# A scheduled four-direction state-space scan on one core: unread products in TensorE's idle stretches, and a limit on second PE stages in a slot

## The chip, the cores and the metric

The kernel runs on one core of a Trainium2 chip. The metric is the device time of one execution in microseconds (us). The engines are called PE (TensorE, with PEld for its weight loads), DVE (VectorE), ACT (ScalarE), POOL (GpSimd) and SP (which issues DMAs here).

## The reference, cut to what matters

The input is 32 images of 128 channels by 32 x 32 points. Four layers are added to it in turn: a 3 x 3 convolution, a Mamba block over four directions, an attention map with two short Mamba blocks, and a small simulated circuit. Nearly all of the time goes to the second layer. Its core, for each direction of each image, is

```
def step(h, inp):
    dt_t, B_t, C_t, u_t = inp
    dA = jnp.exp(dt_t[..., None] * A)
    h = dA * h + (dt_t * u_t)[..., None] * B_t[:, None, :]
    y = jnp.einsum('bdn,bn->bd', h, C_t)
    return (h, y)
```

It runs over 1024 positions with 256 channels (two halves of 128) and 16 states. In front of it stand a projection, a four-tap causal convolution with silu, a projection to B, C and the rate, and a softplus; behind it a skip term, a silu gate and an output projection.

## The kernel before, in words

**Steps.** One direction of one image is a "way" of 32 steps: two halves by 16 states, each step over a 128 x 1024 tile. 32 images give 128 ways, 4,096 steps; the third layer adds 64. `Steps.run` emits one loop iteration per step i, by hand and in this order: on ACT `decay` of step i+3 (L616, the tile `da`); on PE `spread` of step i+1, which puts the row of B into the PSUM tile `bu`; on DVE `scan` (L660, reads `da` and `bu`, writes `hh`) and then `input` of step i+1 (L652, multiplies `bu` by `du`); the stages that the plan hands out; on ACT `scale` for step i+4 (L645); on POOL `weigh` (L669, multiplies `hh` by the row of C, which SP loads as `cc`); and on PE `add` of step i-2 (L705, sums `hh` into `y` by eight transposes).

Two kinds of steps differ in `spread`. In 11 of 32 (`TURNED`) it is eight transposes of `but`, which ACT has scaled (L630), and DVE has no `input`. In the other 21 it is two bf16 products with a selector (L636), and DVE does `input`. `bu` has two buffers, so the products of step i+1 may begin when the scan of step i-1 is done, and the scan of step i+1 needs them one step later: PE's lead over DVE is at most about one step.

**Stages.** All other work of the second layer and its neighbours is cut into `Stage` objects with costs in us for PE, ACT, POOL and DVE: for the next way the projections (`project`, L263), `small` (L282), `keep`, `turn`, `split`, `unturn`, the rate chain (`rate` L360, `expo`, `rounded`, `log`, `lost`, two `whole`, `weighed`), `turns` (L417); for a finished one `gate` (L464), `finish` (L442) and the way out (L1004); for the next image `layer0` with six `conv` stages of 2.6 us of PE (L952). `Plan.slot(i, steps)` is asked once per step. It sorts the streams of stages by slack, and runs at most one stage of each stream if buffers, gaps and a credit per engine allow. `load_of` gives the step's own costs: PE 1.55 us in a plain step, 2.05 with a turned step following, 1.05 more in two steps of 16.

**Buffers.** PE stages write to the PSUM tag `mm`, which has two buffers. Their reading by ACT (or DVE) is held back by `later` and emitted by `flush`, mostly in the next iteration. `mm()` flushes first when two are outstanding[...].

**Tables.** ACT switches between silu and exp/log with a table load: `silu` marks the table as lost, `exps` (L751) loads it again.

## Time and profile before

| | |
|---|---|
| median of 3 runs | 15195.86 us (15194.75 to 15206.05) |
| profiled execution, own time | 15187.89 us |
| its span | 15185.8 us |
| mean granted PE clock | 0.920 |
| busy: DVE, PE, POOL, ACT | 13587.7, 13220.0, 12554.2, 12296.5 us |
| scans (L660) | 4160, 2279 ns each |
| `input` (L652) | 2752, 1212 ns each |
| ACT table loads, L745 and L751 | 481 each, 1283 ns each |

The profile is of one execution. Each engine's row gives its busy time; "idle before" is the engine's time without work ahead of an instruction, with what ended it. PEclk is the clock that PE was granted, as a share of full speed. The span and the execution's own time differ by 2.1 us, which lies outside the first and last instruction.

### The profile page before, as it was taken

What the parts mean: (1) busy time and instruction counts of PE and PEld (TensorE: products, weight loads), DVE (VectorE), ACT (ScalarE), POOL (GpSimd) and SP (SyncE); (2) the same over time, 40 slices, a digit from 0 to 9 for tenths busy, and PEclk for the clock granted to TensorE, in tenths of its full rate; (3) what the DMA queues carried; (4) which work ended last, traced back from release to release, by engine and by line L of the source; (5) the groups of instructions that cost most, each with busy time, mean ns of one, the idle gap of its engine ahead of it and who ended that gap; (6) DMA issues with size and microseconds to landing.
All of it is one profiled execution on the core that took longest, in us unless ns stands there. A gap on an engine that the chain in (4) does not pass through costs nothing.

```text
span 15185.8 us, 197534 instructions
## 1 busy us (share of the span) xinstructions
PE 13220.0 (87%) x70318; PEld 8502.3 (56%) x70318; DVE 13587.7 (89%) x8999; ACT 12296.5 (81%) x21240; POOL 12554.2 (83%) x6433
## 2 busy tenths in 40 slices
PE   7888888888888888888888888888888888888776
PEld 4555555555555555555555555555555555555431
DVE  5999989999999999999899999999999998999887
ACT  6888888888888888888888888888888888888632
POOL 5888888888888888888888888888888888888730
PEclk8999999999999999999999999999999999999877
DMA  3444444444444444444444444444444444444321
GB/s 108 160 156 155 155 153 154 157 158 156 155 156 154 153 156 158 156 156 155 153 153 156 158 156 156 154 155 154 158 159 156 155 156 154 154 159 157 132 96 57
DMA packets 633029, 2277.42 MB, mean 150 GB/s; under 512 B 76808, under 2 KB 80280, under 8 KB 631912
## 3 DMA queue, kind: packets, MB, share of 16 engines
q1 hardware_dynamic: 625128, 2246.09, 42.9%
q0 software_dynamic: 4608, 16.78, 0.3%
q8 instruction: 554, 9.08, 0.2%
q14 instruction: 435, 3.56, 0.1%
q10 hardware_dynamic: 2304, 1.90, 0.0%
HBM read 2221.24 MB, written 43.25 MB: 149 GB/s over the span
## 4 chain that ended last, share of the span: by engine, by line
PE 30%; DVE 24%; ACT 22%; issue 16%; POOL 6%; DMA 1%; DVEq 0%; POOLq 0%; ACTq 0%; SPq 0%
DVE hh L660 14%; DVE bu L652 8%; PE y L705 7%; ACT da L616 7%; ACT but L645 6%; PE mm L263 6%; POOL hh L669 4%; PE bu L636 3%; PE bu L630 3%; PE mm L282 3%; PE mm L952 2%; ACT L751 2%; ACT L745 2%; PE mm L360 1%; PE y L684 1%
## 5 line engine op out<-in xcount | busy, mean ns | idle before, releaser
L669 POOL TENSOR_TENSOR hh<-hh,cc 128x1024 f32<-128x1024 f32 x4160 | 9771.9, 2366 | 1771.3 <-DVE hh L660 1058.4
L660 DVE TENSOR_TENSOR_SCAN hh<-da,bu 128x1024 f32<-128x1024 f32 x4160 | 9411.1, 2279 | 587.1 <-PE bu L630 199.1
L705 PEld LDWEIGHTS y<-cbig,hh 128*128 128x128 f32 x33280 | 4056.6, 150 | 1797.2 <-issue 1264.0
L705 PE MATMUL y<-cbig,hh 128*128 128x128 f32 x33280 | 4754.6, 290 | 194.5 <-POOL hh L669 193.8
L616 ACT ACTIVATE da<-dt,m_na 128x1024 f32<-128x1024 f32 x4096 | 4606.1, 1144 | 329.4 <-DVE hh L660 322.6
L652 DVE TENSOR_TENSOR bu<-du,bu 128x1024 f32<-128x1024 f32 x2752 | 3334.4, 1212 | 747.3 <-PE bu L636 745.7
L645 ACT ACTIVATE but<-dut,bt 128x128 f32<-128x128 f32 x11264 | 3433.6, 392 | 0.0
L636 PE MATMUL bu<-parts,sel 48*128 48x512 bf16 x5504 | 1762.2, 402 | 604.8 <-DVE hh L660 597.0
L263 PE MATMUL mm<-hpad,m_wc 128*128 128x512 f32 x4096 | 2038.6, 621 | 102.4 <-ACT relu L369 68.4
L630 PE MATMUL bu<-cbig,but 128*128 128x128 f32 x11264 | 1613.7, 291 | 379.4 <-DVE hh L660 315.3
L630 PEld LDWEIGHTS bu<-cbig,but 128*128 128x128 f32 x11264 | 1391.7, 152 | 447.7 <-issue 292.0
L263 PEld LDWEIGHTS mm<-hpad,m_wc 128*128 128x128 f32 x4096 | 704.7, 191 | 899.2 <-issue 747.9
L636 PEld LDWEIGHTS <-sel 48*128 48x128 bf16 x5504 | 322.4, 95 | 1115.7 <-DVE hh L660 647.8
L385 POOL TENSOR_TENSOR w<-w,du 128x1024 f32<-128x1024 f32 x260 | 613.8, 2361 | 29.7 <-ACT w L378 29.7
L282 PE MATMUL mm<-uc,m_xw 128*128 128x512 f32 x1024 | 602.4, 719 | 30.4 <-ACT sz L745 21.9
L745 ACT ACT_TABLE_LOAD x481 | 617.1, 1283 | 8.5
L751 ACT ACT_TABLE_LOAD x481 | 617.1, 1283 | 8.5
L422 ACT COPY dut<-mm 128x512 f32<-128x512 f32 x512 | 294.9, 576 | 405.4 <-PE mm L417 405.1
L684 PEld LDWEIGHTS y<-m_skip,uc 128*128 128x128 f32 x4096 | 552.1, 212 | 125.9 <-issue 76.7
L389 POOL TENSOR_TENSOR dt<-dt,w 128x1024 f32<-128x1024 f32 x260 | 615.1, 2366 | 0.3
L394 POOL TENSOR_TENSOR du<-dt,uc 128x1024 f32<-128x1024 f32 x260 | 614.3, 2363 | 0.3
L389 POOL TENSOR_TENSOR dt<-dt,relu 128x1024 f32<-128x1024 f32 x260 | 613.9, 2361 | 0.0
(227 smaller groups left out, 10502.0 us busy)
## 6 DMA issues: line engine op xcount, KB each, us to landing
cc<-rows SPq DMA_DIRECT2D x4160, 512.0 KB, 3.8
xt<-in_x SPq DMA_DIRECT2D x32, 512.0 KB, 5.9
x<-xt SPq DMA_DIRECT2D x32, 512.0 KB, 3.5
xt<-x SPq DMA_DIRECT2D x32, 512.0 KB, 3.5
out<-xt POOLq DMA_DIRECT2D x32, 512.0 KB, 2.9
rows<-dbl SPq DMA_DIRECT2D x130, 64.0 KB, 4.1
stats<-st SPq DMA_DIRECT2D x32, 36.0 KB, 1.5
means<-stats SPq DMA_DIRECT2D x1, 1152.0 KB, 7.1
```

The costliest lines, as they stand in the source:

```text
L263: nc.tensor.matmul(self.view(ps), m.wc[:, v, j, h * P : (h + 1) * P], self.taps(j, c), start=(j == 0), stop=(j == 3),)
L282: nc.tensor.matmul(ps, m.xw[:, h], self.uc[h][:, cs], start=(h == 0), stop=(h == 1))
L389: nc.gpsimd.tensor_tensor(self.dt[h], self.dt[h], t[name], op)
L616: k.nc.scalar.activation(t, w.dt[h], AF.Exp, scale=w.m.na[:, h, n : n + 1])
L630: k.nc.tensor.matmul(t[:, b * P : (b + 1) * P], but[:, b], k.ident, start=True, stop=True, is_transpose=True,)
L636: k.nc.tensor.matmul(t[:, cs], k.sel[:, n], w.parts[:, cs], start=True, stop=True)
L645: k.nc.scalar.activation(t[:, b], w.dut[h][:, b], AF.Copy, scale=w.bt[:, b, n : n + 1])
L652: k.nc.vector.tensor_tensor(t, w.du[h], t, ALU.mult)
L660: k.nc.vector.tensor_tensor_scan(way(t), way(self.da.pop(i)), way(self.bu.pop(i)), 0.0, ALU.mult, ALU.add)
L669: k.nc.gpsimd.tensor_tensor(t, t, self.cc.pop(i), ALU.mult)
L705: k.nc.tensor.matmul(self.y[g][: w.bl, b], t[:, at], k.ident, start=False, stop=(n == DS - 1 and b == w.per - 1), is_transpose=True,)
L745: self.nc.scalar.activation(*args, AF.Silu, **kw)
```

## The change

Three things are new. `Plan.slot` keeps `busy`, the costs of the step and of the stages handed out in it, and passes over a stage if a PE stage is already in the slot, if the sum for PE would go over 3.6 us, and if its stream has slack over 1.2. It returns PE's and DVE's sums. `Steps.run` keeps `late`, an account of PE's lag: PE's sum less 1.1 times DVE's, never below zero after an iteration. At the end of an iteration, when the account says that PE is ahead by more than 1.2 us, `Kernel.idle` issues products of 48 x 512 bf16 that nothing reads, one for each 0.25 us of the rest, into a buffer of the tag `mm`, unless two users of that tag are outstanding.

```diff
--- before.py
+++ after.py
...
         self.credit = [min(c + self.SLOT - own, self.SLOT) for c, own in zip(self.credit, steps)]
+        busy = list(steps)
...
             stage = s["left"][0]
+            if slack(s) > 1.2 and busy[0] > steps[0] and busy[0] + stage.cost[0] > 3.6:
+                continue
             if i < max(stage.at, s["last"] + stage.gap):
                 continue
...
             self.credit = [c_ - c for c, c_ in zip(stage.cost, self.credit)]
+            busy = [b + c for b, c in zip(busy, stage.cost)]
...
+        return busy[0], busy[3]
...
+        late = 0.0
         for i in range(len(steps) + 2):
...
             if self.has(i):
-                plan.slot(i, self.load_of(i))
+                pe, dve = plan.slot(i, self.load_of(i))
+                late += pe - 1.1 * dve
             self.scale(i + 4)
             self.weigh(i)
             self.add(i - 2)
+            if self.has(i + 2):
+                late += k.idle(-late - 1.2)
+            late = max(late, 0.0)
             self.load(i + 3)
...
+    def idle(self, us):
+        each = 0.25
+        n = int(us / each)
+        if n < 1 or len(self.waiting) + len(self.behind) + self.open + bool(self.single) > 1:
+            return 0.0
+        ps = self.psm.tile([P, 512], F32, tag="mm", name="unread")
+        for _ in range(n):
+            self.nc.tensor.matmul(
+                ps, self.half[: 3 * DS], self.sel[:, :4].rearrange("p n d -> p (n d)"),
+                start=True, stop=True,
+            )
+        return n * each
```

## The prediction

> **What bounds the kernel now.** I read the page's busy shares and clock row first, then who waited for whom, then stretches and the timeline of one image.

> ```profile
> PE 13220.0 (87%) x70318; PEld 8502.3 (56%) x70318; DVE 13587.7 (89%) x8999; ACT 12296.5 (81%) x21240; POOL 12554.2 (83%) x6433
> PEclk8999999999999999999999999999999999999877
> ...
> DVE bu L652 <- PE bu L636: 745.7, 519, 87.2
> DVE hh L660 <- PE bu L630: 199.1, 170, 3.2
> ...
> PE y L705 <- POOL hh L669: 193.8, 181, 3.0
> ```

> DVE paces the loop. By the timeline a plain step lasts 3.54 us and one before a turned step 2.20, with no wait in it; 32 steps (21 and 11) make 98.6 us, an image 394. Scans of the trace are 442 us apart per image, so 48 us of an image are something else: about 21 us of other DVE work and some 27 us in which DVE waits for PE. The two DVE rows say so: less the one wait of 87.2 us, which lies outside the images, they are 857 us, 27 per image. This is the prize, 860 us at most. The tenths of the clock row hide that PE ran at half speed for a part of it: the mean is 0.92.

> The waits come in clusters. Two of them, in one image (times on the left, waits in brackets):

> ```profile
> 2448.94:2457.19 8.25, 4.65 (x25) 2.31 (x24) 8.08 (x8) 7.77 (x15) 7.19 (x4) 0.91 0.54 191
> 2457.19:2469.81 12.62, 12.62 (x55) 8.42 (x56) 9.32 (x8) 4.43 (x11) 12.38 (x8) 0.78 0.29 96
> ...
> 2455.99 1.03 PE L636 MATMUL bu<-parts,sel 48*128 48x512 bf16 x2 [3.08 <-DVE hh L660]
> 2456.95 3.78 PE L282 MATMUL mm<-uc,m_xw 128*128 128x512 f32 x4
> 2460.81 2.98 PE L684 MATMUL y<-m_skip,uc 128*128 128x128 f32 x16
> 2464.36 1.23 DVE L652 TENSOR_TENSOR bu<-du,bu 128x1024 f32<-128x1024 f32 x1 [1.23 <-PE bu L636]
> ...
> 2549.70 0.33 PE L442 MATMUL mm<-cbig,carry 128*128 128x128 f32 x1 [2.28 <-ACT uc L745]
> 2555.54 1.12 PE L360 MATMUL mm<-dbl,m_dw 32*128 32x512 f32 x2 [1.51 <-ACT dut L422]
> 2556.59 0.30 PEld L952 LDWEIGHTS mm<-xpad,w 128*128 128x128 f32 x2 [0.76 <-ACT relu L369]
> 2560.87 1.23 DVE L652 TENSOR_TENSOR bu<-du,bu 128x1024 f32<-128x1024 f32 x1 [5.92 <-PE bu L636]
> ```

> First: in two slots without PE stages (2448.94 to 2457.19) PE is busy 4.65 of 8.25 us; then the clock is down to 0.78, L282 takes 3.78 us (four of them at full speed about 2.0), and DVE waits. Second: a slot got `turn`, `rate` and a `conv` at once. Each in turn waits until ACT has read one of the two `mm` buffers: 2.28 + 1.51 = 3.8 us of PE, and the third one's weight load 0.76 (its product starts right behind the one before). DVE then waits 5.92.

> [...] I cut it into the stretches of 3.41 us in which its clock changes, and took each product's array time from the spacing of its like (0.109 us for 128 f32 columns, 0.216 for 512 bf16). Of 221 stretches at full clock in which the array was filled under 40%, 204 were followed by half clock; from 40 to 50%, 41%; above 80% practically none of 2,152. Back to full it goes only from a well filled stretch: none of 132 under 70%, 81% of 399 above 80%. A plain slot without a stage fills 8 x 0.109 + 2 x 0.216 = 1.30 of 3.54 us, 37%: it is just too empty. [...] of 440 stretches in which other products filled under a tenth, only 22% were followed by half clock. [...]

> **The change, part by part.** The built program shows what the plan does.

> *Unread products.* 2,520 of them, in 799 of 4,160 slots, mostly four at a time. The nearest row is L636, with the same 48 x 512 bf16: spacing 0.216 us at full clock, 0.43 at half. So 2,520 x 0.216 = 544 us more of PE, 17 us per image. Four add 0.86 us: the plain empty slot goes from 37 to 61% filled, out of the zone that surely lowers the clock. They stand at the end of an iteration, behind `add`, ahead of the next `spread`; that one waits for a scan's end anyway (L636 <- DVE was 3.08 us above), and this wait covers them. Without that cover they would cost what they last, up to 0.86 us a slot.

> *The limit of 3.6.* Slots with two or more PE stages fall from 725 to 500, slots with over 3.6 us for PE from 1,137 to 916. PE's work per image is unchanged (374 us of stage costs). As projections also run closer together, ACT's pairs of table loads fall from 481 to 420: 122 x 1.283 = 157 us off ACT, which is not the bound. I count 0 for it, and up to 30 us, because DVE rows that wait for ACT are small (`but` 15.6 us). Nothing is added to SP's or POOL's queues; POOL's rate chain only moves by some slots. `keep`, whose DMA writes the rows that `cc` loads read, moves from slot 7 to 8 or from 5 to 9 of a way and is needed in slot 29.

> *By cluster of an image.* Slots are counted from the image's first step; "before" is DVE's wait for PE, averaged over 30 images; "after" is what PE's sum leaves over DVE's pace less one step of lead, with half a microsecond where a low clock is still possible.

> - 19 to 26: 4.35, 4.35, 3.80, 3.30 in a row, then 4.20, 3.80, 3.30; now 4.35, 4.35, 2.05, 3.30. Before 2.9, after 0.4.
> - 32 to 36: two empty slots, then 4.65 and 5.25 at half clock; now 3.30, 3.30, 4.35, 2.90, 2.05, never empty. Before 2.6, after 0.2.
> - 45: before 1.1; now filled, after 0.4.
> - 52 to 57: before 1.8, after 0.1.
> - 60 to 71, six `conv`: before 10.7, of which about 4 are the buffer waits. Now one `conv` has a slot with at most a `turn`, so these go. But the delayed projections now meet the `conv`: PE's sum is 49.8 us, DVE's pace 37.1 plus 1.5 for two L964; 11.2 less a step's lead of 3.5 leaves 7.7. With something for buffers, after 8.5.
> - 72 to 83: before 5.6. The account still says that PE lags there (by up to 9.6 us in slot 71, although DVE has waited that off), so nothing is filled and the clock may fall. After 4.
> - 91 to 94, 103 to 104, 123 and smaller ones: before 3.3, after 1.1.

> Sum before 28, after 14.7. For new waits that I don't see I take 2.5: 10.8 us less per image, times 31.5 (the first image lacks some) 340 us. From the profiled execution's 15187.9 us that gives 14,848; the median of the runs stands 8 us higher, so 14,855.

> **Rivals.** A change of 0.2%, 30 us, is about what a measurement of this kernel can tell from none.

> *Levelling and clock both work, as above:* 14,680 to 15,000. Chance 0.45.

> *The fillers don't hold the clock:* 61% is in the band (50 to 80%) in which about one stretch in nine still led to half clock, and slots with one filler stay near 43%. Then the limit alone works: of 13.3 us saved about 7 per image without the clusters at 33, 45, 91 and 123: 14,970. Chance 0.16.

> *Waits move instead of going:* PE's work is the same, and the conv cluster grows. If slots 60 to 83 take back 7 to 8 of the other clusters' 9.5 us, 15,100 remains (0.15 for a gain of over 30 us), or nothing (0.07). For it: 49.8 us of PE there against 44.4 before.

> *Slower, by fillers in the way:* the account takes costs at full clock and knows nothing of POOL. `add` waits for POOL (193.8 us in 181 times), the fillers stand behind it, and the next `spread` behind them; at half clock four of them last 1.7 us. It decides from the point where 340 of their 544 us, 63%, are no longer covered. If all are in the way the time is 15,195.9 + 544 - 340 = 15,400; with most of them and a grown conv cluster, 15,300. Against it: they are given only where the slot has over a microsecond to spare, and DVE's scan was what PE waited for in 912 us (L636 597.0, L630 315.3). Chance 0.17.

> **The numbers.** Likeliest 14,855, own range 14,680 to 15,000. The range for 8 in 10 reaches over the second and third cases into no change and the mildest losses: 14,680 to 15,220. Faster 0.45 + 0.16 + 0.15 = 0.76, same 0.07, slower 0.17.

> **What would show it.** Right: L652's wait for L636 falls from 746 to some 450 us and L630's row from 199 to about 100; granted clock 0.95 or more; 420 table loads per line; PE busy higher by about 500 us and DVE's unchanged; the unread products idle or overlapped ahead of L636's wait for the scan, which shrinks by their length. Wrong: DVE's waits for PE at 850 us or more with a high clock (waits moved, or fillers in the way: then `bu` comes late behind L774); clock unchanged at 0.92 with unread products present[...]; or DVE's wait passing to ACT or POOL, whose stage costs per image (408 and 394 us) are close to DVE's 416.

## The result: slower by 0.8%, and the profile after

The changed kernel takes 15315.44 us (median of 4 runs, 15290.75 to 15335.65), the kernel before 15195.31 us; the ratio is 1.0079, with a 95% interval of 1.006 to 1.0098. The forecast was 14,855 us. The profiled execution's span is 15325.0 us, 139 more than before. Lines have moved: L652 is now L663, L660 is L671, L636 is L647, L630 is L641, L705 is L716, L669 is L680; the unread products are L774.

From the page after, busy shares and the granted clock:

```profile
PE 13703.6 (89%) x72838; PEld 8618.8 (56%) x72838; DVE 13622.9 (89%) x8999; ACT 12150.9 (79%) x21118; POOL 12569.3 (82%) x6433
PEclk8999999999999999999999999999999999999877
```

And who waited for whom (total, times, longest):

```profile
DVE bu L663 <- PE bu L647: 747.2, 427, 86.9
DVE hh L671 <- PE bu L641: 273.6, 225, 3.6
...
PE y L716 <- POOL hh L680: 393.1, 332, 2.9
```

PE is busy 484 us more, about what 2,520 products cost. But DVE's waits for PE are what they were (745.7 us before) or longer (199.1 before), the mean clock is 0.93 instead of 0.92, and PE waits twice as long for POOL. Of the forecast's signs only the products' time and the 420 table loads came true.

The two clusters that the forecast showed are now these stretches: slots 32 and 33, 34 to 36, and 60 to 64 of the image; then its slots 66 to 71 and 27 to 30 (columns as before: length, busy time of PE, PEld, DVE, ACT, POOL, then the clock):

```profile
2471.25:2479.55 8.30, 7.98 (x33) 3.92 (x32) 8.13 (x7) 6.27 (x13) 5.89 (x4) 1.00 0.41 134
2479.55:2488.90 9.35, 6.49 (x53) 5.62 (x52) 9.08 (x8) 8.56 (x15) 9.33 (x5) 1.00 0.36 113
2566.10:2591.33 25.23, 21.68 (x92) 11.97 (x91) 16.37 (x10) 16.99 (x28) 16.90 (x10) 0.93 0.42 142
2594.88:2619.65 24.77, 24.77 (x121) 14.92 (x120) 19.09 (x12) 17.54 (x30) 20.78 (x9) 1.00 0.40 132
2449.80:2467.72 17.92, 15.07 (x80) 9.47 (x80) 14.30 (x8) 14.26 (x24) 16.70 (x9) 0.90 0.53 201
```

The kernel before has for slots 27 to 30 and 66 to 71:

```profile
2430.76:2445.41 14.65, 12.15 (x74) 8.06 (x72) 14.23 (x9) 11.94 (x16) 12.09 (x7) 1.00 0.66 228
2578.86:2599.23 20.37, 17.68 (x97) 12.20 (x96) 19.94 (x15) 13.68 (x26) 19.83 (x9) 0.92 0.38 127
```

The first cluster is gone, at full clock (9.35 us in place of 12.62). The conv slots gained 2 us (27.35 before). Slots 66 to 71 take 24.77 us with PE busy throughout; before they took 20.37. And slots 27 to 30 take 17.92 us, before 14.65. In the timeline this last one reads:

```profile
2453.22 1.09 PE L716 MATMUL y<-cbig,hh 128*128 128x128 f32 x8 [2.85 <-POOL hh L680]
2454.24 1.03 PE L774 MATMUL unread<-sel,half 48*128 48x512 bf16 x4
2455.20 1.95 PE L641 MATMUL bu<-cbig,but 128*128 128x128 f32 x8
2457.28 2.29 DVE L671 TENSOR_TENSOR_SCAN hh<-da,bu 128x1024 f32<-128x1024 f32 x1 [1.66 <-PE bu L641]
```

`add` waits 2.85 us for POOL, four unread products follow (1.03 us), and `spread` then takes 1.95 us at a granted clock of 0.50 (the same eight took 1.04 us at 2444.88, at a clock of 1.00). DVE waits 1.66 us for it. This is what the forecast's rival "slower, by fillers in the way" (chance 0.17, 15,300 to 15,400 us) describes, so the first suspicion was that the products simply lie in the way.

### The profile page after: what moved, and what is told of

Same layout as the page of the kernel before. It is cut to its first block, busy times and chain, and to the rows that moved or that the text cites. A ratio compares the mean times of both kernels' runs of the same rounds, so it can differ in the third digit from the quotient of the medians.

```text
span 15325.0 us, 202407 instructions
## 1 busy us (share of the span) xinstructions
PE 13703.6 (89%) x72838; PEld 8618.8 (56%) x72838; DVE 13622.9 (89%) x8999; ACT 12150.9 (79%) x21118; POOL 12569.3 (82%) x6433
## 4 chain that ended last, share of the span: by engine, by line
PE 30%; DVE 29%; issue 16%; ACT 15%; POOL 10%; DVEq 0%; DMA 0%; POOLq 0%; ACTq 0%; SPq 0%
DVE hh L671 18%; DVE bu L663 8%; PE y L716 7%; POOL hh L680 6%; ACT da L627 5%; ACT but L656 4%; PE mm L263 4%; PE mm L978 3%; PE bu L647 3%; PE bu L641 3%; PE unread L774 2%; POOL dt L389 2%; POOL du L394 2%; PE mm L360 1%; PE mm L282 1%
## 5 line engine op out<-in xcount | busy, mean ns | idle before, releaser
L680 POOL TENSOR_TENSOR hh<-hh,cc 128x1024 f32<-128x1024 f32 x4160 | 9782.6, 2367 | 1880.8 <-DVE hh L671 1077.6
L671 DVE TENSOR_TENSOR_SCAN hh<-da,bu 128x1024 f32<-128x1024 f32 x4160 | 9409.0, 2280 | 704.8 <-PE bu L641 273.6
L716 PEld LDWEIGHTS y<-cbig,hh 128*128 128x128 f32 x33280 | 3982.1, 148 | 1959.2 <-issue 1170.5
L716 PE MATMUL y<-cbig,hh 128*128 128x128 f32 x33280 | 4648.2, 286 | 401.3 <-POOL hh L680 393.1
L663 DVE TENSOR_TENSOR bu<-du,bu 128x1024 f32<-128x1024 f32 x2752 | 3338.1, 1213 | 759.7 <-PE bu L647 747.2
L647 PE MATMUL bu<-parts,sel 48*128 48x512 bf16 x5504 | 1726.4, 395 | 511.2 <-DVE hh L671 497.1
L263 PE MATMUL mm<-hpad,m_wc 128*128 128x512 f32 x4096 | 2003.0, 612 | 3.2 <-ACT relu L369 2.2
L641 PE MATMUL bu<-cbig,but 128*128 128x128 f32 x11264 | 1629.1, 292 | 151.4 <-DVE hh L671 111.1
L641 PEld LDWEIGHTS bu<-cbig,but 128*128 128x128 f32 x11264 | 1360.2, 151 | 423.9 <-issue 232.9
L647 PEld LDWEIGHTS <-sel 48*128 48x128 bf16 x5504 | 351.1, 95 | 1033.4 <-issue 547.1
L774 PE MATMUL unread<-sel,half 48*128 48x512 bf16 x2520 | 784.1, 427 | 1.9 <-DVE sz L448 1.7
L422 ACT COPY dut<-mm 128x512 f32<-128x512 f32 x512 | 296.7, 579 | 469.6 <-PE mm L417 468.9
L695 PEld LDWEIGHTS y<-m_skip,uc 128*128 128x128 f32 x4096 | 516.0, 200 | 167.2 <-issue 69.8
L978 PE MATMUL mm<-xpad,w 128*128 128x512 f32 x1152 | 552.9, 618 | 47.9 <-ACT xpad L965 47.7
L695 PE MATMUL y<-m_skip,uc 128*128 128x128 f32 x4096 | 531.2, 285 | 44.1 <-ACT carry L734 44.1
```

What stands on the lines that cost most here:

```text
L263: nc.tensor.matmul(self.view(ps), m.wc[:, v, j, h * P : (h + 1) * P], self.taps(j, c), start=(j == 0), stop=(j == 3),)
L641: k.nc.tensor.matmul(t[:, b * P : (b + 1) * P], but[:, b], k.ident, start=True, stop=True, is_transpose=True,)
L647: k.nc.tensor.matmul(t[:, cs], k.sel[:, n], w.parts[:, cs], start=True, stop=True)
L663: k.nc.vector.tensor_tensor(t, w.du[h], t, ALU.mult)
L671: k.nc.vector.tensor_tensor_scan(way(t), way(self.da.pop(i)), way(self.bu.pop(i)), 0.0, ALU.mult, ALU.add)
L680: k.nc.gpsimd.tensor_tensor(t, t, self.cc.pop(i), ALU.mult)
```

## The experiments

### Which half of the change loses

Four kernels. The first drops the call of `idle`, the second drops the limit, the third and fourth issue the products ahead of `scale`, `weigh` and `add`, with and without the limit.

```diff
 # limit alone
-            if self.has(i + 2):
-                late += k.idle(-late - 1.2)
 # products alone
-            if slack(s) > 1.2 and busy[0] > steps[0] and busy[0] + stage.cost[0] > 3.6:
-                continue
 # products ahead of add (with the limit, and without)
+            if self.has(i + 2):
+                late += k.idle(-late - 1.2)
             self.scale(i + 4)
             self.weigh(i)
             self.add(i - 2)
-            if self.has(i + 2):
-                late += k.idle(-late - 1.2)
```

> The limit of 3.6 us alone, no unread products. Theory A (the loss is the limit's: it moves rate chains, gates and projections so that POOL and ACT lag elsewhere and six conv stages meet projections): as slow as the changed kernel, 15,300 us or more, with the new clusters of waits in slots 28, 29, 49, 82, 83, 93, 94 of an image still there. Theory B (the loss is the unread products', which stand behind an add that waits for POOL and ahead of the next spread): faster than the kernel before, about 14,970 us, as the forecast had it for the limit alone.

> The unread products alone (3,003 of them, as the plan without the limit leaves more idle slots by its account), no limit. Theory A: below 15,100 us, since the kernel before loses at least 6 us an image where the clock falls, and its schedule is kept. Theory B: 15,300 us or more, DVE waiting for spreads that come right behind unread products.

> The changed kernel with the unread products issued ahead of the iteration's scale, weigh and add instead of behind them, so that they run while add waits for POOL. Theory B: the direct cost goes (in the changed kernel the trace allows at most 126 us of DVE waits to be filler time) and PE's stretches of waiting for POOL are no longer empty, so the clock rises over 0.93: about 15,150 us. Theory A: within 40 us of the changed kernel, 15,280 to 15,330.

> Unread products alone, issued ahead of add, no limit. Theory A and B both: the fastest of the four, about 15,000 us, if the low clock costs what the rows of the kernel before say; about 15,195 us if the low clock is a sign of idle time and not a cost.

| | median us | ratio to before (95%) | clock |
|---|---|---|---|
| limit alone | 15188.83 | 0.9996 (0.9988 to 1.0005) | 0.933 |
| products alone (3,003) | 15307.18 | 1.0079 (1.0066 to 1.0091) | 0.938 |
| both, products ahead of `add` | 15282.29 | 1.0061 (1.0048 to 1.0073) | 0.933 |
| products alone, ahead of `add` | 15323.49 | 1.0093 (1.0079 to 1.0107) | 0.935 |

The limit alone makes no difference, where theory B had 14,970 us; all of the loss is the products'. Theory A falls. Theory B has the right half, but not the right reason: moved out from behind `add`, with the limit, the products still cost 93 us over the limit alone, and without it they cost as much as behind it (the two intervals overlap). I had expected 15,150 and 15,000 us. What was odd was the clock. With the limit, 2,520 fillers leave it where the limit alone has it (0.930 and 0.933). Without the limit, 3,003 of them raise it from 0.920 to 0.938, and the kernel is slower all the same.

### Why the clock does not rise

I sorted the 3.41 us stretches of the changed kernel's trace again, by whether they hold unread products. At full clock and 40 to 50% filled, 35 of 36 stretches with such products were followed by half clock, but 32% of 154 without. At half clock and over 90% filled, 39% of 124 with them went back to full clock, and 84% of 157 without. (Such counts move with how a product's time is laid into the stretches. Laid end to end from the recorded starts they are 31 of 40 against 40% of 115, and 31% of 160 against 76% of 262; the order is the same.) At the same fill, then, the stretches with unread products had the lower next clock.

A count that takes in the rows sorts the stretches better. Take one limit on the fill at full clock and one at half clock, and forecast each next clock of a trace with them. With plain array time the best limits are wrong in 341 of 4,441 stretches of the kernel before, and in 376 of 4,482 of the changed kernel. With each product's time multiplied by its rows / 128 they are wrong in 88 and 61; the best limits on this weighted fill are about 0.38 at full clock and 0.75 at half clock in both traces.

A count doesn't prove a cause, so the rows were changed and the length, number and places of the products kept:

```diff
 # 128 rows (the same identity tile as weights and, four times, as the moving side)
-                ps, self.half[: 3 * DS], self.sel[:, :4].rearrange("p n d -> p (n d)"),
+                ps.rearrange("p (n d) -> p n d", d=P), self.half,
+                self.half.unsqueeze(1).to_broadcast([P, 4, P]),
 # 16 rows
-                ps, self.half[: 3 * DS], self.sel[:, :4].rearrange("p n d -> p (n d)"),
+                ps, self.half[:DS], self.sel[:DS, :4].rearrange("p n d -> p (n d)"),
```

> The changed kernel, its unread products over 128 rows instead of 48 (a 128 x 128 bf16 tile as weights and, four times over, as the moving side); as many, as long and in the same places. Theory R ([...] a regression over the 3.41 us stretches of four traces gives 48-row products a weight of 0.32 to 0.45 against 1 for 128-row ones): a plain slot goes from 39 to 54% weighted, the clock rises to 0.96 or more, stretches at half clock fall from 50 to below 20 us an image, and the time falls by 100 to 200 us, to about 15,150 us. Theory D (the unread products cost because they lie in PE's way, whatever the clock does): clock and time as in the changed kernel within 40 us, 15,280 to 15,350.

> The changed kernel, its unread products over 16 rows. Theory R: [...] the clock is below the changed kernel's 0.934, at 0.92 or less, and the time is over 15,340 us. Theory D: as the changed kernel, 15,280 to 15,350 us, and the same clock.

> 128-row unread products without the limit of 3.6 us. Theory R: clock 0.96 or more, and 15,307 us of the 48-row version falls to about 15,100 us, below the kernel before. Theory D: 15,280 to 15,340 us.

> 128-row unread products, with the limit, issued ahead of scale, weigh and add. Theory R: clock 0.96 or more and the fastest of the four, about 15,080 us, as they then run while add waits for POOL. Theory D: 15,260 to 15,310 us, as the 48-row version of it (15,282).

| unread products | median us | ratio to before (95%) | clock |
|---|---|---|---|
| none (limit alone) | 15188.83 | 0.9996 (0.9988 to 1.0005) | 0.933 |
| 2,520 of 16 rows, limit | 15437.62 | 1.0158 (1.0144 to 1.0172) | 0.917 |
| 2,520 of 48 rows, limit (the change) | 15315.44 | 1.0079 (1.006 to 1.0098) | 0.93 |
| 2,520 of 128 rows, limit | 15153.22 | 0.9969 (0.9957 to 0.998) | 0.945 |
| the same, ahead of `add` | 15137.1 | 0.9956 (0.9943 to 0.997) | 0.949 |
| 3,003 of 128 rows, no limit | 15134.86 | 0.9957 (0.9945 to 0.997) | 0.957 |

With the instruction stream the same but for rows, the time goes from 15,438 over 15,315 to 15,153 us. DVE's waits for PE fall with it, from 33.2 over 28.4 to 23.6 us an image. Theory R stands and theory D falls, since the products of the three kernels last as long as each other (medians of 374, 376 and 379 ns). The number format is no rival: the products are bf16 in all three. The rows of the tile `unread` give the duration of one product in ns (minimum, median, maximum); with 48 rows they are 372, 376 and 631. With 16 rows:

```profile
L774 PE MATMUL unread<-sel,half x2520: 371/374/630, 132.3 to 14851.6; 16*128 16x512 bf16 x194
```

With 128 rows:

```profile
L774 PE MATMUL unread<-half x2520: 376/379/635, 130.3 to 14546.4; 128*128 128x512 bf16 x194
```

In slots 27 to 30 of the same image the stretch with 16 rows is:

```profile
2449.69:2470.85 21.16, 18.30 (x65) 10.87 (x65) 14.31 (x8) 15.37 (x24) 16.64 (x9) 0.60 0.50 170
```

With 128 rows:

```profile
2419.28:2435.66 16.38, 13.10 (x80) 8.48 (x80) 14.29 (x8) 14.61 (x24) 16.08 (x9) 1.00 0.58 194
```

With the limit alone:

```profile
2426.48:2441.68 15.20, 11.84 (x66) 8.64 (x67) 14.21 (x8) 14.30 (x24) 15.07 (x8) 0.89 0.56 188
```

And the timeline with 16 rows, where the clock is low:

```profile
2453.09 1.21 PE L716 MATMUL y<-cbig,hh 128*128 128x128 f32 x8 [2.86 <-POOL hh L680]
2454.24 1.88 PE L774 MATMUL unread<-sel,half 16*128 16x512 bf16 x4
2464.51 1.23 DVE L663 TENSOR_TENSOR bu<-du,bu 128x1024 f32<-128x1024 f32 x1 [4.07 <-PE bu L647]
```

With 16 rows the clock is 0.60 over the whole stretch: the four products last 1.88 us (1.03 at a clock of 1.00, in the changed kernel's timeline above), and DVE waits 4.07 us for PE ten microseconds later. With 128 rows the clock is 1.00 there; the 1.2 us over the limit alone (16.38 and 15.20) is what the products themselves still cost in this place. Over 30 images DVE waits for PE in slots 27 to 31 for 7.4, 5.2 and 2.7 us with 16, 48 and 128 rows, and 2.1 without products.

The expected clock of 0.96 was missed (0.945 to 0.957), though the times came within 60 us. Time at half clock fell from 50 to 40 us an image with 128 rows in the changed kernel, not below 20 as expected; the kernel before has 59 and the limit alone 47.

### Where the limit's gain goes, and a better version

DVE's waits per image, averaged over 30 images, by slot (for PE; the sum for ACT and a stage of DVE's own work in the last rows):

| slots | before | limit alone | both (the change) |
|---|---|---|---|
| 18 to 26 | 2.8 | 0.7 | 0.2 |
| 27 to 31 | 0.3 | 2.1 | 5.2 |
| 32 to 38 | 2.6 | 0.0 | 0.1 |
| 51 to 57 | 1.7 | 0.3 | 0.1 |
| 58 to 65 | 10.3 | 7.7 | 7.3 |
| 66 to 71 | 0.0 | 3.3 | 3.3 |
| 72 to 83 | 5.6 | 4.5 | 3.4 |
| all 128, for PE | 27.4 | 24.4 | 28.4 |
| all 128, for ACT | 2.2 | 3.8 | 3.4 |
| DVE's `means` stage itself | 2.4 | 4.1 | 3.5 |

The limit does what the forecast said in slots 18 to 26, 32 to 38 and 51 to 57, and gives most of it back in 27 to 31, 66 to 71 and for ACT. The rest, 1.7 us an image, is DVE's own work, and all of it is the `means` stage, two operations on 128 x 64 elements of the tile `st`, for the third layer. Their work is the same; what changes is how long they last, and those over 0.4 us end just behind an instruction of POOL (below). In slots 27 to 31 PE's waits for POOL went from 0.0 to 2.9 us an image with the limit alone: the limit moved work of the rate chain on POOL into slots 26 and 27 (2.6 to 4.8 us in the two). In slots 66 to 71 of the limit alone PE is busy without a gap, as in the changed kernel:

```profile
2570.94:2595.71 24.77, 24.77 (x121) 14.93 (x120) 19.09 (x11) 17.52 (x30) 20.77 (x9) 1.00 0.41 132
```

Four more kernels asked whether this is the projections' doing, and whether the account's imagined lag (up to 9.6 us behind the conv stages, which DVE has waited off by then) keeps slots from being filled. The cap was set on the account, the limit was set in a part of an image's slots.

```diff
 # limit in slots 0 to 31 only, no products
-            if slack(s) > 1.2 and busy[0] > steps[0] and busy[0] + stage.cost[0] > 3.6:
+            if i % 128 < 32 and slack(s) > 1.2 and busy[0] > steps[0] and busy[0] + stage.cost[0] > 3.6:
 # account capped (128 rows, no limit)
-            late = max(late, 0.0)
+            late = min(max(late, 0.0), 1.5)
 # account capped and limit in slots 32 to 63
+            if 32 <= i % 128 < 64 and slack(s) > 1.2 and busy[0] > steps[0] and busy[0] + stage.cost[0] > 3.6:
 # the same, products from 0.6 us to spare
-                late += k.idle(-late - 1.2)
+                late += k.idle(-late - 0.6)
```

> The limit of 3.6 us in slots 0 to 31 of an image's 128 only, no unread products. Theory M (the limit's gain is given back because the projections that it puts off meet the six conv stages): the waits of slots 18 to 26 fall from 2.8 to about 0.7 us an image and those of slots 66 to 71 rise from 0 to about 5 (PE and ACT), so the time is 15,200 to 15,290 us, not faster than before. Rival: the loss of the limit alone is spread over other slots; then this is faster than before by the 2 us an image of slots 18 to 26, about 15,130 us.

> 128-row unread products without the limit (as e7), the account of PE's lag never above 1.5 us, so that slots after the conv stages are filled too (3,439 products in place of 3,003). Theory R, and that the account carries lag which DVE has already waited off: half-clock time falls from 27 to below 20 us an image, time 15,134.9 us falls by 10 to 50 us. Theory D: more products in the way, 15,150 us or more.

> As e10, with the limit in slots 32 to 63 of an image only, where it takes the lump of slots 34 and 35 apart and by the plan's costs adds nothing to the conv stages. Theory M: 20 to 50 us below e10, the fastest so far. Rival: the pieces only move, within 15 us of e10.

> As e11, with products already from 0.6 us of spare time in the account instead of 1.2 (5,872 products in place of 3,311). Theory R: clock 0.97 or more; if the time then doesn't fall below e11's, what is left of the low clock costs nothing and the products in the way do: then 15,120 us or more.

| | median us | ratio to before (95%) | clock |
|---|---|---|---|
| limit in slots 0 to 31, no products | 15373.41 | 1.0118 (1.0104 to 1.0132) | 0.924 |
| 128 rows, capped account (3,439) | 15049.15 | 0.9904 (0.9891 to 0.9918) | 0.963 |
| the same, limit in slots 32 to 63 (3,311) | 15006.09 | 0.9877 (0.9862 to 0.9892) | 0.960 |
| the same, from 0.6 us to spare (5,872) | 15099.08 | 0.9939 (0.9927 to 0.9952) | 0.960 |

Ratios are to the kernel before as it ran beside each group (15,192 to 15,201 us), so differences across tables are good to about 10 us.

*Early limit.* It alone brings the waits in slots 66 to 71 (3.3 us for PE and 1.9 for ACT, where 5 were expected), with slots 18 to 26 down to 0.8: the exchange is shown. It loses 181 us, more than either expectation had; another 3.4 us an image come up in slots 106 to 120 and 1.7 in 121 to 127. The largest of these, 2.0 us in slot 115, reads like this in one image: a projection waits 2.21 us until ACT has read an `mm` buffer, runs at a low clock (0.70), and DVE waits 4.33 us. Why the early limit puts it there was not followed.

```profile
2760.72 2.72 PE L263 MATMUL mm<-hpad,m_wc 128*128 128x512 f32 x4 [2.21 <-ACT relu L369]
2766.72 1.23 DVE L661 TENSOR_TENSOR bu<-du,bu 128x1024 f32<-128x1024 f32 x1 [4.33 <-PE bu L645]
```

*Capped account.* It gains 86 us, more than the 10 to 50 expected. DVE's waits for PE fall from 25.1 to 20.9 us an image, 2.8 of these 4.2 us in slots 72 to 105, behind the conv stages. Time at half clock falls from 27 to 21 us an image, just short of the 20 expected.

*Limit in slots 32 to 63.* It takes off 43 us more, as expected, but not for the reason given. DVE's waits for PE don't fall. With the capped account alone, then with this limit too (the best version, 15006.09 us, 1.2% under the kernel before; in kernels without the limit or with other products the lines stand a few apart):

```profile
DVE bu L661 <- PE bu L645: 621.7, 398, 86.9
DVE hh L669 <- PE bu L639: 120.1, 120, 3.2
```

```profile
DVE bu L663 <- PE bu L647: 667.3, 423, 87.3
DVE hh L671 <- PE bu L641: 109.0, 114, 3.5
```

By slot they go from 0.5 to 0.0 us in 32 to 38 and from 10.5 to 9.0 in 58 to 65, but from 3.9 to 5.1 in 72 to 83 and from 1.0 to 1.9 in 84 to 105. What falls is DVE's own busy time, from 13618.1 to 13570.6 us, and that is `means` again (3.80 to 2.35 us an image). Its two operations, with the capped account alone and then with the limit (ns: minimum, median, maximum):

```profile
L1079 DVE TENSOR_SCALAR st<-st x32: 247/2228/2383, 703.6 to 14145.8; 128x64 f32<-128x64 f32 x32
L1080 DVE TENSOR_SCALAR st<-st x32: 255/2199/2207, 705.9 to 14146.6; 128x64 f32<-128x64 f32 x32
```

```profile
L1081 DVE TENSOR_SCALAR st<-st x32: 230/2258/2510, 709.7 to 14094.9; 128x64 f32<-128x64 f32 x32
L1082 DVE TENSOR_SCALAR st<-st x32: 254/256/400, 712.3 to 14095.7; 128x64 f32<-128x64 f32 x32
```

So that expectation was met by luck: the second operation takes 0.256 us in the median, where it took 2.199. The best version's lead over the kernel before doesn't rest on it (`means` takes 2.39 us an image there), but on 5.9 us an image less of waiting for PE.

*More products.* The clock stays at 0.960, where 0.97 was expected, and the time rises by 93 us, with DVE's waits for PE up from 21.5 to 25.8 us an image: from here on they only lie in the way.

## Why the prediction was wrong

*The filling of a plain slot.* The step that failed is "four add 0.86 us: the plain empty slot goes from 37 to 61% filled". It counted the array's time, whatever a product's rows. Weighted by rows the slot has, by an estimate from the prediction's spacings (0.109 and 0.216 us), 0.87 + 0.375 x 0.43 = 1.03 of 3.54 us, 29%, and four fillers add 0.375 x 0.86 = 0.32: 38%, just on the limit of 0.38 that sorts the two traces best, and less with fewer fillers. The rows were in the trace's forms (48x512 next to 128x128), and the same sorting of stretches by kind would have shown it before the run. The runs show it: PE spends 47 us an image at half clock with the limit alone and 50 with the 48-row products added. The forecast's second case, that the fillers don't hold the clock, had this; but it priced them at nothing then.

*"This wait covers them."* Not at half clock: the products of a low stretch take 0.43 us each (by the prediction's spacing), and of the 124 low stretches that held them and were over 90% filled only 39% were followed by full clock. The limit alone takes 15188.83 us and the change 15315.44: 127 us, about 4 us an image, where 0 was set.

*The limit.* Forecast at 7 us an image by itself, measured 0.1 in the distance between scans (48.0 to 47.9 us over the floor of 394): 3.0 us less of waiting for PE, but 1.6 more for ACT and 1.7 more in `means`, neither of which was counted. The single clusters were right; slots 60 to 71 were not: forecast 8.5, measured in the change, for slots 58 to 71, 10.6 for PE and 1.9 for ACT. The 2.5 us for new waits were short: slots 27 to 31 alone have 5.2. What was overlooked there is POOL: PE's waits for it doubled to 393.1 us, and the limit alone has them too (414.7). Moving the rate chain "by some slots" was not free.

*The rival "slower, by fillers in the way"* had the sign, the place (products behind an `add` that waits for POOL) and, in part by luck, the size. As a mechanism it covers a small part at most: out from behind `add` the change gains 33 us of 127, and the intervals of the two overlap. How the rest divides between time in the way and the lower clock that goes with it isn't measured; that rows alone turn it into a gain of 36 us over the limit alone is.

*Right:* the clock's two levels (1.0 and 0.5, the only ones in the clock records of both traces) and their effect (0.216 and 0.43 us for a product), 484 us of PE, table loads, the clusters in 18 to 26 and 32 to 38, and the account's error behind the conv stages, where the capped account gained most.

## What to carry to other kernels

Look at the rows of products that are only to keep TensorE's clock up: here the same number, length and places gave +1.6%, +0.8% and -0.3% with 16, 48 and 128 rows. An account of an engine's lag has to forget lag that another engine has waited off, and a limit on one engine's load is to be judged by where the displaced work goes next, on all engines. A gain of the size expected is not yet the gain expected: look it up in the waits that it was to shorten. Before filling, sort the trace's stretches by clock and kind of work: here forecasts of the next clock from time weighted by rows were wrong in 88 stretches of the kernel before, where those from time alone were wrong in 341.

## What the runs showed of the hardware

DVE's two `means` operations on 128 x 64 elements take from about 0.23 to 4.6 us each with the same work. In the traces of the kernel before and of the changed one every one of the 31 and 52 that last over 0.4 us ends 49 to 58 ns after a `weigh` on POOL ends. With the capped account, in one image:

```profile
2454.48 2.23 DVE L1079 TENSOR_SCALAR st<-st 128x64 f32<-128x64 f32 x1
2456.82 2.20 DVE L1080 TENSOR_SCALAR st<-st 128x64 f32<-128x64 f32 x1
2454.28 4.69 POOL L678 TENSOR_TENSOR hh<-hh,cc 128x1024 f32<-128x1024 f32 x2
```

DVE's scans last 2.24 to 2.31 us each in the kernel before and `input` 1.20 to 1.24 us, with POOL busy for 83% of the span. Why the one kind of operation varies so and the other doesn't was not tested.
